# Reversing the order of the query blocks and starting the first group's first pass by chunks

## The chip, the core and the metric

The kernel runs on one core of a Trainium2 chip. The metric is the device time of one execution in microseconds (us), from the first to the last instruction and the little around them. A core has five engines that run side by side: TensorE (PE: matrix multiplies, with weight loads shown as PEld), VectorE (DVE), ScalarE (ACT), GpSimd (POOL) and SyncE (SP), which here only issues DMA transfers, in the order in which they are written. The profiler also records the clock that the chip grants to TensorE, as a share of full speed; in these traces it is either 1.0 or 0.5 at any moment, and means over a stretch lie between.

## The reference

Two layers over two sequences of 2048 tokens with 256 channels. What matters here is the first layer: a differential attention (16 heads, each a difference of two causal softmaxes with 8 channels) beside a mixture of experts (8 routed experts, two for each token, and one shared expert), both on the normalised input. The second layer (a state-space scan and a network with weights of plus and minus one) is not touched by the change.

```python
x = L0_attn_x                                   # (2, 2048, 256)
xn = _layernorm(x, axis=-1)
x = x + _L0_attn_ref(xn, ...) + _L0_ffn_ref(xn, ...)
xn = _layernorm(x, axis=-1)
x = x + _L1_attn_ref(xn, ...) + _L1_ffn_ref(xn, ...)
# in _L0_attn_ref
qkv = x @ w_attn
att = jnp.einsum('bhtd,bhsd->bhts', q, k) * (1.0 / math.sqrt(hd))
att = jnp.where(causal, att, -jnp.inf)
att = jax.nn.softmax(att, axis=-1)
att = att[:, :, 0] - lambda_full * att[:, :, 1]
out = jnp.einsum('bhts,bhsd->bhtd', att, v)
```

## The kernel before

Everything about the first layer is in `layer0`. A **block** is 512 tokens; a sequence `b` has four, T = 0 to 3, so there are eight, numbered 4b + T. A **group** is one block and one eighth of the heads (four score matrices, two heads). Causality makes a group of block T look at T + 1 blocks of keys ("chunks"): its keys are 4T + 4 tiles of 128. So there are 64 groups, and 2 x 8 x (4 + 8 + 12 + 16) = 640 steps of the second pass. One such step, a **unit**, is four score multiplies (L467), four exponentials on ACT (L474), and four multiplies with the values (L493, "av"). A unit is also the clock of the hand-written plan: `at` counts units.

Softmax needs the maximum of each row first. That is the **first pass** (`first_pass`): score multiplies with queries as weights (L395), the mask added by small bf16 multiplies on the diagonal (L409, "halves"), and a maximum on DVE over PSUM (L416). The negative maxima are turned (L432) and sent by a DMA into a row of the query tile, where the second pass adds them. The first pass of a group is spread over the units of the group before it.

`place(begin, end, steps)` spreads steps over a stretch of units; `until(time)` releases them between the scores. The order on PE and SP is exactly this order; the other engines are ordered by the tile framework. What is placed beside the attention:

- `prepare(blk)`: load a block of x, statistics, normalise, eight transposes, the router's logits (L271), and a store to `xnT`. Before: block 0 at the start, the others at units 4 blk - 7 to 4 blk - 3.
- `project_qk(b, T)` and `project_v(b, T)`: the projections of a block, just before its first group. Queries and keys are split into two float32r parts in a tile `parts` of one buffer (L318, L319), stored to a scratch (L325) and loaded again by groups (`load`, L367 and L372).
- `project_out`: the output projection of a block when its last group is done, added to x and stored in `x1`.
- `route()` and `scatter(n)`: the choice of experts at units 30 to 44, and the scatter of rows at units 46 to 108.
- `expert_steps()`: 55 jobs of 256 rows, 16 of the shared expert and 39 of routed ones, each five "visits" long (L809 up and gate, L831 down; together "MoE", all with the PSUM tile `moe`). Their visits are spread evenly from unit `BEGIN` = 48 to the end: 1320 multiplies, each two instructions in the trace. Four shared jobs (of the last two blocks) come after the routed ones.
- `gather(pair)`: near the end, for each of 16 pairs of tiles, an indirect DMA by POOL (L926) fetches the routed results and DVE adds them.

`NSH = NBLK - 2` marks the two blocks (6 and 7) whose shared jobs come last; block 7 (`NBLK - 1`) ends the layer, with its sum held in the tile `late`. After unit 640, `project_out` of the last block and the statistics end the layer; then the weights of layer 1 are loaded (`load_branch`, `load_signs`) and `layer1` runs.

Of the kernel before, what the change touches and what calls it, by code (L numbers as in the profile page):

```python
# [37 lines left out]
@with_exitstack  # L38
def block_kernel(ctx: ExitStack, tc: tile.TileContext, t: dict, out: bass.AP):
    nc = tc.nc  # L40

    x = t["L0_attn_x"]
    B, S, C = x.shape
    NT = B * S
    NTILE = NT // P
    out_t = out.flatten_outer_dims().rearrange("(n p) c -> p n c", p=P)


    const = ctx.enter_context(tc.tile_pool(name="const", bufs=1))
# [24 lines left out]

    def behind():
        normalisation(0, NTILE - 4)
        pool = w1p.enter_context(tc.tile_pool(name="w1", bufs=1, side="right"))
        load_branch(tc, t, pool, ident, w1)

    layer0(tc, t, x, x1, mv, rstd, ident, eps, behind)  # L80
    normalisation(NTILE - 4, NTILE)


    pool = w1p.enter_context(tc.tile_pool(name="w1f", bufs=1, side="right"))
    layer1(tc, t, B, S, x1, shift, rstd, ident, w1, out_t, lambda: load_signs(tc, t, pool, w1))
    w1p.close()


def layer0(tc, t, x, x1, mv, rstd, ident, eps, ended):
# [31 lines left out]
    with ExitStack() as ctx:  # L121
# [4 lines left out]
        def load_x(key, blk=None):  # L126
            blk = key if blk is None else blk
            xbs[key] = new(sp, [P, 4, C], "xb")
            nc.sync.dma_start(xbs[key], x_t[:, 4 * blk : 4 * blk + 4, :])

        load_x(0)
        load_x(1)
# [102 lines left out]
        def prepare(blk):  # L235
# [29 lines left out]
            def logits():  # L265
# [3 lines left out]
                for i in range(4):  # L269
                    for k in range(KC):  # L270
# [7 lines left out]
                if blk:  # L278
# [17 lines left out]
            for b in range(B)  # L296
        }

        def project_qk(b, T):

            blk = b * NTB + T
            heads = P // HD
# [21 lines left out]
                    d = dst[:, :, part] if n == "q" else dst[:, part]  # L324
                    nc.sync.dma_start(d, parts[:, part].bitcast(F32))  # L325

            return [lambda n=n, e=e: one(n, e) for e in range(KC) for n in "kq"]

        vas = {}

# [194 lines left out]
        def project_out(b, T, out):  # L525
# [3 lines left out]

            def scale():  # L530
                xbs[blk] = late
                if blk < NBLK - 1:
# [31 lines left out]
            def project(i):  # L564
                pt = new(ps1, [P, 2, 512], "s1")[:, 0]
                for k in range(KC):
                    nc.tensor.matmul(
                        pt[:, :C],
                        oTs[i][:, k * P : (k + 1) * P],
                        wo[:, k, :],  # L570
                        start=(k == 0),
                        stop=(k == KC - 1),
                    )
                acc = xbs[blk][:, i, :]
                nc.vector.tensor_tensor(acc, acc, pt[:, :C], ALU.add)
                if blk == NBLK - 1:
                    statistics(4 * blk + i, acc)

            def store():
                nc.sync.dma_start(x1[:, 4 * blk : 4 * blk + 4, :], xbs.pop(blk))  # L580
                projected.add(blk)

            steps = [scale]
            steps += [lambda: turn(0)]
# [2 lines left out]
            return steps + [store]  # L587


        stored, projected, begun = set(), set(), []  # L590
        NSH = NBLK - 2

        def statistics(n, acc):
            st = new(sp, [P, nc.vector.BN_STATS_DIM], "bnst", bufs=3)
# [161 lines left out]
        def expert_steps():  # L756
# [95 lines left out]
            def load_base(jb):  # L852
                n = GT * jb["j"]
                begun.append(n // 4)
                jb["c"] = new(mps[0], [P, GT, C], "c", bufs=2)
                src = x1 if n // 4 in projected else x_t
                nc.sync.dma_start(jb["c"], src[:, n : n + GT, :])
# [9 lines left out]

            def finish(jb):
                n = GT * jb["j"]
                if n // 4 < NBLK - 1:  # L870
                    for i in range(GT):
                        statistics(n + i, jb["c"][:, i, :])

            order = [dict(j=j, shared=True, last=False) for j in range(2 * NSH)]
            order += [dict(j=j, shared=False) for j in range(NJ)]
            order += [dict(j=j, shared=True, last=True) for j in range(2 * NSH, 2 * NBLK)]
            v = 0
            for i, jb in enumerate(order):
                names = ("gate", "up"), ("down",)
                begins = jb["j"] == (2 * NSH if jb.get("last") else 0)  # L880
                if not jb["shared"]:
                    if begins:
                        put(v, to_routed)
# [26 lines left out]
        def gather(pair):  # L910
# [1 line left out]
            n = GT * pair  # L912

            def load():
                if n // 4 < NBLK - 1:
# [19 lines left out]
            def add():  # L935
                for i in range(GT):
                    acc = pairs[pair][:, i, :]
                    for o in range(2):
# [4 lines left out]
                    if n // 4 < NSH:  # L943
                        statistics(n + i, acc)

            return load, add, (lambda: store_last(pair)) if n // 4 < NSH else None

        def store_last(pair):
            n = GT * pair
            acc = pairs.pop(pair)  # L950
            if n // 4 < NBLK - 1:
                nc.sync.dma_start(x1[:, n : n + GT, :], acc)

        pairs = {}
# [4 lines left out]
        LEAD, FETCH = 3, 2  # L959
        groups, at = [], 0  # L960
        for b in range(B):
            for T in range(NTB):
                for g in range(NG):
                    groups.append(dict(b=b, T=T, g=g, at=at, n=4 * T + 4))
                    at += 4 * T + 4
# [8 lines left out]
        for i, grp in enumerate(groups):  # L974
# [673 lines left out]
```

## Time and profile before

| | us |
|---|---|
| median of 9 runs | 4181.72 (4155.36 to 4214.71) |
| the profiled execution | 4169.49 |
| its span | 4167.8 |
| first second-pass score at | 77.5 |
| end of the attention, about | 2894.5 |
| first scan of layer 1, about | 2973 |

A "windows" view gives, for stretches of the span, how long each engine was busy (with the number of instructions), the mean granted clock and the DMA share; filtered by a line or a tile it counts those instructions alone. Counting L467 (four for each unit) tells which stretch of time holds which units: units 0 to 47 lie in 77.5 to 393.7 (193 of L467), the same 48 units of the second sequence (320 to 367) in 1527.4 to 1759.2 (192), units 528 to 591 in 2442.5 to 2673.9 (256), and the last 48 in 2673.9 to 2894.5 (192). A busy PE is not a fast PE: at half the clock the same multiply is busy about twice as long.

### The profile page before, as it was taken

The page shows a single profiled execution, that of the slowest core. Times are in us where ns is not written, and L with a number is a line of the kernel's source. Part 1 is how long each engine was busy: PE and PEld are TensorE (multiplying, and loading weights), DVE is VectorE, ACT ScalarE, POOL GpSimd, SP SyncE. Part 2 cuts the span into 40 slices and gives each one's busy share as a digit, 9 for nine tenths or more (in the row PEclk, how much of TensorE's full clock was granted, in tenths as well). Part 3 has the DMA queues.
Part 4 walks back from the last instruction along what each step waited for, and adds up shares of the span by engine and source line. Part 5 has one row for each costly group of instructions (what it writes and reads, how often), then busy time and mean ns, then how long its engine had stood idle before and what let it go on. Part 6 is the DMA issues. An engine that isn't in the chain of part 4 may idle for free. (4 is left out here: it accounts for less than half of the span.)

```text
span 4167.8 us, 58041 instructions
## 1 busy us (share of the span) xinstructions
PE 3726.0 (89%) x20976; PEld 1994.8 (48%) x20976; DVE 2771.0 (66%) x3758; ACT 2329.8 (56%) x4766; POOL 1488.7 (36%) x1859
## 2 busy tenths in 40 slices
PE   6789999999999999999999999987487887878888
PEld 3444444544444445554454454443254544545545
DVE  4355576756676535656666667673488888888888
ACT  2334444645665554555565556544575775776674
POOL 2112332101000022111110100142587887888887
PEclk7556997998999999999999999988698888889989
DMA  3322321112122322222222222332322322321331
GB/s 103 103 75 79 108 92 58 52 57 79 64 87 65 100 74 93 74 87 88 70 84 89 67 72 79 98 103 64 124 75 78 112 86 72 114 93 64 122 102 41
DMA packets 219022, 348.70 MB, mean 84 GB/s; under 512 B 31968, under 2 KB 118496, under 8 KB 218736
## 3 DMA queue, kind: packets, MB, share of 16 engines
q1 hardware_dynamic: 212048, 327.68, 23.8%
q0 software_dynamic: 6144, 16.79, 1.2%
q8 instruction: 167, 2.74, 0.3%
q14 instruction: 119, 0.97, 0.1%
q10 hardware_dynamic: 544, 0.52, 0.0%
HBM read 261.93 MB, written 82.31 MB: 83 GB/s over the span
## 5 line engine op out<-in xcount | busy, mean ns | idle before, releaser
L416 DVE TENSOR_REDUCE mpart<-s 128x2 f32<-128x1024 f32 (+3 forms) x1280 | 1353.0, 1064 | 667.8 <-PE s L467 335.0
L474 ACT ACTIVATE pr<-s 128x512 f32<-128x512 f32 (+3 forms) x2560 | 1248.8, 532 | 923.6 <-PE s L467 636.7
L467 PE MATMUL s<-qst,kc 34*128 34x512 f32 (+3 forms) x2560 | 1022.0, 466 | 42.9 <-ACT pr L474 28.3
L395 PE MATMUL s<-kc,qst 33*128 33x512 f32 (+3 forms) x2560 | 946.5, 449 | 50.0 <-DVE mpart L416 27.3
L478 POOL TENSOR_SCALAR_AFFINE_SELECT pr<-pr 128x128 f32<-128x128 f32 x1024 | 290.9, 293 | 1617.2 <-ACT pr L474 1604.4
L395 PEld LDWEIGHTS s<-kc,qst 33*128 33x128 f32 x2560 | 432.1, 203 | 744.1 <-issue 319.9
L493 PE MATMUL av<-pr,va 128*17 128x512 f32 (+3 forms) x5120 | 653.8, 582 | 4.6 <-POOL pr L478 4.6
L1519 POOL TENSOR_TENSOR u<-dxr,bc 128x1024 f32<-128x1024 f32 x256 | 601.6, 2371 | 12.5 <-DMA bc<-bcd 12.5
L467 PEld LDWEIGHTS s<-qst,kc 34*128 34x128 f32 x2560 | 448.2, 200 | 171.5 <-ACT pr L474 98.8
L1532 ACT ACTIVATE a<-dtr,w_A 128x512 f32<-128x512 f32 x512 | 350.7, 691 | 169.0 <-DVE u L1579 150.2
L1418 PEld LDWEIGHTS f<-h,w_f 128*128 128x128 f32 x2048 | 262.1, 196 | 102.3 <-issue 35.0
L1579 DVE TENSOR_TENSOR_SCAN a<-a,state,u 128x512 f32<-128x512 f32 x240 | 307.0, 1279 | 3.6 <-ACT a L1532 2.7
L1418 PE MATMUL f<-h,w_f 128*128 128x256 f32 x2048 | 288.6, 297 | 16.2 <-ACT h L1425 9.3
L409 PE MATMUL s<-halves 64*128 64x128 bf16 x2048 | 288.7, 242 | 0.0
L809 PE MATMUL moe<-xT,w_up 128*128 128x256 f32 x880 | 266.6, 428 | 0.0
L809 PE MATMUL moe<-xT,w_gate 128*128 128x256 f32 x880 | 265.7, 427 | 0.0
L1418 PE MATMUL f<-xhl,w_f 128*128 128x256 f32 x512 | 121.6, 368 | 133.8 <-DVE h L1429 99.4
L1585 DVE TENSOR_TENSOR u<-a,bc 128x512 f32<-128x512 f32 x320 | 221.4, 692 | 14.4 <-DVE a L1579 0.5
L1593 POOL TENSOR_TENSOR u<-u,bc 128x1024 f32<-128x1024 f32 x96 | 227.1, 2366 | 7.7
L831 PE MATMUL moe<-w_down,hT 128*128 128x256 f32 x880 | 224.2, 399 | 0.0
L1544 PE MATMUL y<-u,w_sel 128*32 128x512 f32 x1024 | 190.1, 655 | 33.4 <-POOL u L1593 27.7
L519 POOL TENSOR_TENSOR ao<-n 128x128 f32<-128x128 f32 x64 | 29.4, 459 | 526.8 <-DVE n L516 526.0
(196 smaller groups left out, 4196.9 us busy)
## 6 DMA issues: line engine op xcount, KB each, us to landing
kc<-kd SPq DMA_DIRECT2D x640, 64.0 KB
dxr<-dtd SPq DMA_DIRECT2D x64, 512.0 KB
dtr<-dtd SPq DMA_DIRECT2D x64, 512.0 KB
w_gate<-in_L_ffn_gate_proj_w SPq DMA_DIRECT2D x39, 512.0 KB
w_up<-in_L_ffn_up_proj_w SPq DMA_DIRECT2D x39, 512.0 KB
w_down<-in_L_ffn_down_proj_w SPq DMA_DIRECT2D x39, 512.0 KB
qst<-qd SPq DMA_DIRECT2D x256, 64.0 KB
bc<-bcd SPq DMA_DIRECT2D x32, 512.0 KB
```

The costliest lines, as they stand in the source:

```text
L395: nc.tensor.matmul(pt[:, i, :width], grp["q"][r : r + R + 1, pair, tt * P : (tt + 1) * P], grp["k"][ch][r : r + R + 1, pair, :width], star ...
L409: nc.tensor.matmul(pt[:, head, tt * P : width], halves[h, 0, half, :], halves[h, 1, half, :], start=False, stop=half == 1,)
L416: nc.vector.tensor_reduce(grp["mpart"][:, tt, 2 * pair : 2 * pair + 2, ch : ch + 1], pt[:, :, :width], AX.X, ALU.max,)
L467: nc.tensor.matmul(pt[:, lo:], grp["k"][st // 4][r : r + R + 2, pair, (st % 4) * P : (st % 4 + 1) * P], grp["q"][r : r + R + 2, pair, lo:] ...
L474: nc.scalar.activation(pr[:, j, lo:], pt[:, lo:], AF.Exp)
L478: nc.gpsimd.affine_select(out=block, in_=block, compare_op=ALU.is_ge, fill=0.0, base=0, pattern=[[1, P]], channel_multiplier=-1,)
L493: nc.tensor.matmul(av[32 * j : 32 * j + DV + 1, lo:], vas[b, st // 4][:, st % 4, 2 * g + j // 2, :], pr[:, j, lo:], start=(st == 0), stop= ...
L809: nc.tensor.matmul(moe[:, half, :], w[:, k, m * P : (m + 1) * P], jb["xT"][:, k, :], start=(k == 0), stop=(k == KC - 1),)
L1418: nc.tensor.matmul(pt, w[wname][:, k, m * P : (m + 1) * P], h[src][:, k, part, :], start=(k + part == 0), stop=(k + 1 + part == nk + 1),)
L1519: nc.gpsimd.tensor_tensor(u, sg["dxr", c, half], sg["bc", g][:, 0:1, :].to_broadcast([P, 2, L]), ALU.mult)
L1532: nc.scalar.activation(a, sg["dtr", c, half][:, i, :], AF.Exp, scale=w["A"][:, k : k + 1])
L1579: nc.vector.tensor_tensor_scan(h, a, u[:, i, :], sg["before"]["state"][:, k[i] : k[i] + 1] if sg["before"] else 0.0, ALU.mult, ALU.add,)
```

## The change

The plan is rearranged; the multiplies, exponentials and maxima are the same in number and shape.

- The blocks of each sequence run T = 3, 2, 1, 0. So the first group of a sequence needs the keys of all four blocks.
- For sequence 0 the beginning is new: block 3 is prepared and its q and k projected, then for T = 0, 1, 2 the block is prepared and its k projected, and the first group's first pass runs by chunks in between. v of all four blocks and q of blocks 0 to 2 are placed beside that first pass (which reads the blocks again from `xnT` with `load_xT`).
- The four blocks of sequence 1 are prepared at units 2 to 21 and projected at units 190, 212, 236 and 293, over 16 units each.
- The expert visits begin at unit -10 in place of 48.
- The blocks whose shared jobs come last are now 4 and 5 (T = 0 and 1 of sequence 1): `LAST` and `NEXT`. The order of the gathers follows.
- The second layer's normalisation is made in three pieces in place of two.

```diff
     def behind():
-        normalisation(0, NTILE - 4)
+        normalisation(0, 16)
+        normalisation(20, NTILE)
...
-        def project_qk(b, T):
+        def project_qk(b, T, names="kq"):
...
-            return [lambda n=n, e=e: one(n, e) for e in range(KC) for n in "kq"]
+            return [lambda n=n, e=e: one(n, e) for e in range(KC) for n in names]
...
-        NSH = NBLK - 2
+        LAST, NEXT = NBLK - NTB, NBLK - NTB + 1
+        ended_by = [LAST, NEXT]
...
-            order = [dict(j=j, shared=True, last=False) for j in range(2 * NSH)]
+            ends = [GT * blk + i for blk in ended_by for i in range(2)]
+            order = [dict(j=j, shared=True, last=False) for j in range(2 * NBLK) if j not in ends]
             order += [dict(j=j, shared=False) for j in range(NJ)]
-            order += [dict(j=j, shared=True, last=True) for j in range(2 * NSH, 2 * NBLK)]
+            order += [dict(j=j, shared=True, last=True) for j in ends]
...
         for b in range(B):
-            for T in range(NTB):
+            for T in reversed(range(NTB)):
...
-                b, T = grp["b"], grp["T"]
                 grp["out"] = {}
-                before = project_qk(b, T) + project_v(b, T)
-                start = begin - FETCH - 2 - 2 * len(before)
-                place(start, begin - FETCH - 2, before)
-                if i:
-                    place(start - 3, start - 3, [lambda blk=b * NTB + T: load_xT(blk)])
...
-                place(end + 5, end + 14, project_out(grp["b"], grp["T"], grp["out"]))
-
-        place(-60, -59, prepare(0))
-        for blk in range(1, NBLK):
-            place(4 * blk - 7, 4 * blk - 3, prepare(blk))
+                soon = (grp["b"], grp["T"]) == (B - 1, 1)
+                place(end + 5, end + (10 if soon else 14), project_out(grp["b"], grp["T"], grp["out"]))
+
+        last = NTB - 1
+        for i, T in enumerate([last] + list(range(last))):
+            start = 4 * max(i - 2, 0) + (-22 if i > 1 else 2 * i - 40)
+            place(start, start + 0.5, prepare(T))
+            place(start + 0.5, start + 1, project_qk(0, T, "kq" if T == last else "k"))
+            start = 4 * T - 15
+            place(start, start, [lambda T=T: load_xT(T)])
+            place(start + 0.5, start + 3.5, project_v(0, T) + (project_qk(0, T, "q") if T < last else []))
+            place(5 * i + 2, 5 * i + 6, prepare(NTB + last - i))
+        for T, start in enumerate((190, 212, 236, 293)):
+            place(start - 3, start - 3, [lambda blk=NTB + T: load_xT(blk)])
+            place(start, start + 16, project_qk(1, T) + project_v(1, T))
...
-        BEGIN = 48
+        BEGIN = -10
...
-        pairs_order = [12, 0, 1, 2, 13, 3, 4, 14, 5, 6, 15, 7, 8, 9, 10, 11]
+        pairs_order = [8, 0, 1, 2, 3, 9, 4, 5, 6, 7, 12, 13, 14, 15, 10, 11]
...
+            if pair // 2 == NEXT:
+                time = at - 20.5 + pair % 2
```

More of the change, by code (lines that the diff above doesn't have):

```diff
@@ L80, in block_kernel @@
     layer0(tc, t, x, x1, mv, rstd, ident, eps, behind)
-    normalisation(NTILE - 4, NTILE)
+    normalisation(16, 20)
     pool = w1p.enter_context(tc.tile_pool(name="w1f", bufs=1, side="right"))
@@ L129, in load_x @@
             nc.sync.dma_start(xbs[key], x_t[:, 4 * blk : 4 * blk + 4, :])
+        load_x(NTB - 1)
         load_x(0)
-        load_x(1)
         wqk = new(wp, [P, KC, 2 * C], "wqk")
@@ L277, in logits @@
                         )
-                if blk:
+                if blk >= NTB:
                     xTs.pop(blk)
@@ L531, in scale @@
                 xbs[blk] = late
-                if blk < NBLK - 1:
+                projecting.add(blk)
+                if blk != LAST:
                     assert begun.count(blk) == 2 * (blk in stored)
@@ L575, in project @@
                 nc.vector.tensor_tensor(acc, acc, pt[:, :C], ALU.add)
-                if blk == NBLK - 1:
+                if blk == LAST:
                     statistics(4 * blk + i, acc)
@@ L581, in store @@
                 projected.add(blk)
+                projecting.remove(blk)
             steps = [scale]
@@ L587, in project_out @@
             return steps + [store]
-        stored, projected, begun = set(), set(), []
-        NSH = NBLK - 2
+        stored, projected, projecting, begun = set(), set(), set(), []
+        LAST, NEXT = NBLK - NTB, NBLK - NTB + 1
+        ended_by = [LAST, NEXT]
         def statistics(n, acc):
@@ L854, in load_base @@
                 begun.append(n // 4)
+                assert n // 4 not in projecting
                 jb["c"] = new(mps[0], [P, GT, C], "c", bufs=2)
@@ L869, in finish @@
                 n = GT * jb["j"]
-                if n // 4 < NBLK - 1:
+                if n // 4 != LAST:
                     for i in range(GT):
                         statistics(n + i, jb["c"][:, i, :])
-            order = [dict(j=j, shared=True, last=False) for j in range(2 * NSH)]
+            ends = [GT * blk + i for blk in ended_by for i in range(2)]
+            order = [dict(j=j, shared=True, last=False) for j in range(2 * NBLK) if j not in ends]
             order += [dict(j=j, shared=False) for j in range(NJ)]
-            order += [dict(j=j, shared=True, last=True) for j in range(2 * NSH, 2 * NBLK)]
+            order += [dict(j=j, shared=True, last=True) for j in ends]
             v = 0
@@ L879, in expert_steps @@
                 names = ("gate", "up"), ("down",)
-                begins = jb["j"] == (2 * NSH if jb.get("last") else 0)
+                begins = jb["j"] == (ends[0] if jb.get("last") else 0)
                 if not jb["shared"]:
@@ L914, in load @@
             def load():
-                if n // 4 < NBLK - 1:
+                if n // 4 != LAST:
                     assert n // 4 in projected
@@ L942, in add @@
                         )
-                    if n // 4 < NSH:
+                    if n // 4 not in ended_by:
                         statistics(n + i, acc)
-            return load, add, (lambda: store_last(pair)) if n // 4 < NSH else None
+            return load, add, (lambda: store_last(pair)) if n // 4 not in ended_by else None
         def store_last(pair):
@@ L950, in store_last @@
             acc = pairs.pop(pair)
-            if n // 4 < NBLK - 1:
+            if n // 4 != LAST:
                 nc.sync.dma_start(x1[:, n : n + GT, :], acc)
```

## The prediction, made before the changed kernel was run

> **What bounds the kernel now.** I read the page's slices first, then the windows by stage, then the start's timeline. Of the 40 slices (104 us each), this is PE, its granted clock, and DVE:
>
> ```profile
> PE   6789999999999999999999999987487887878888
> ...
> DVE  4355576756676535656666667673488888888888
> ...
> PEclk7556997998999999999999999988698888889989
> ```
>
> PE is the full engine from slice 4 to slice 26, the first layer. But in slices 1 to 3 it is 70 to 90% busy at about half the clock. The windows give that by stage (columns: stretch, its length, busy us and instructions of PE, PEld, DVE, ACT and POOL, granted clock, DMA share, GB/s):
>
> ```profile
> 0.00:77.50 77.50, 41.59 (x167) 25.07 (x167) 34.45 (x67) 9.94 (x18) 18.01 (x35) 0.79 0.29 93
> 77.50:393.70 316.20, 271.06 (x1326) 142.33 (x1325) 150.28 (x299) 121.24 (x257) 54.50 (x173) 0.54 0.26 86
> ...
> 1527.40:1759.20 231.80, 218.41 (x1449) 122.79 (x1448) 130.04 (x203) 113.24 (x265) 58.76 (x180) 0.91 0.30 92
> ...
> 2442.50:2673.90 231.40, 229.68 (x1489) 114.14 (x1488) 164.28 (x193) 147.79 (x306) 19.86 (x68) 1.00 0.24 78
> 2673.90:2894.50 220.60, 194.63 (x989) 89.08 (x992) 119.25 (x236) 109.50 (x218) 76.44 (x113) 0.84 0.33 96
> ```
>
> Rows two and three hold the same 48 units of the two sequences: 316.2 us against 231.8, although the later ones carry MoE too. Row four is the dense stretch: 64 units, PE busy throughout, full clock. Two more windows, of all instructions:
>
> ```profile
> 393.70:2894.50 2500.80, 2402.57 (x14582) 1208.77 (x14586) 1552.19 (x2084) 1377.28 (x2905) 419.56 (x1079) 0.93 0.25 80
> 626.00:671.00 45.00, 39.72 (x158) 18.62 (x158) 19.50 (x29) 17.09 (x30) 15.57 (x20) 0.51 0.20 68
> 172.00:380.00 208.00, 187.62 (x894) 98.91 (x891) 104.42 (x208) 79.53 (x168) 36.22 (x111) 0.50 0.23 79
> ```
>
> From 172 to 380 PE was busy 187.62 of 208 us, at half clock all the while, and rose when MoE began. So PE's being busy is not what raises the clock here; multiplies that fill the array are (MoE 128x128; the scores have 33 or 34 rows, the values 17 columns). MoE alone, by the same windows:
>
> ```profile
> 77.50:393.70 316.20, 0.00 (x0) 0.00 (x0) 0.00 (x0) 0.00 (x0) 0.54 0.26 86
> 1527.40:1759.20 231.80, 62.60 (x213) 39.68 (x212) 15.51 (x37) 10.26 (x27) 0.91 0.30 92
> ```
>
> **The sum.** The built orders hold the same PE work, so I ask what it costs where it now stands. Unit prices at full clock, from starts to next starts in the timeline (instructions of the trace): MoE .24 us (four from 2600.46 to 2601.43), q or k projection .48 (four from 2210.30 to 2212.21), v projection .27 (four from 2249.78 to 2250.85), transpose .13 (four from 2601.43 to 2601.96), score .14 and mask .07 (four each from 2601.96 to 2602.79). A logit instruction took .22 at half clock (14 in 3.15 us), so .11.
>
> *1. MoE from unit -10: the clock of the first units.* 231.8 less 213 MoE at .24 (51) is 181 without MoE. The first 48 units of before also held six preparations (48 transposes, 96 logits: 17 us) and lacked seven sets of four routed turns (4 us): 194. They took 316: **-122** for running this work at the later clock. MoE itself is moved, not added. Bounds: -142 (also the rest of the clock, 0.91 to 1.00) and -60 (half of the early units still slow).
>
> *2. The longer start.* The timeline of before:
>
> ```profile
> 32.10 0.60 ACT L318 ACTIVATE parts<-s 128x512 fp32r<-128x512 f32 x1 [3.19 <-PE s L310]
> 36.36 0.60 ACT L318 ACTIVATE parts<-s 128x512 fp32r<-128x512 f32 x1 [3.66 <-DMA kd<-parts]
> 39.86 0.60 ACT L318 ACTIVATE parts<-s 128x512 fp32r<-128x512 f32 x1 [2.90 <-DMA qd<-parts]
> ...
> 48.71 0.60 SPq L372 DMA_DIRECT2D kc<-kd  x1
> ...
> 53.87 0.57 PE L395 MATMUL s<-kc,qst 33*128 33x128 f32 x2 [5.26 <-DMA kc<-kd]
> ```
>
> A projection waits for the store of the one before, as `parts` has one buffer: 4 us each. A first score waits 5.2 us for its chunk. In the changed order, before the first chunk's loads SP stands behind eight projections: four of block 3 (32 to 48), two of block 0 (to 58), then block 1's x is loaded only behind those stores (3), gets its statistics and is normalised (4.6, as from 17.4 to 22.0 before), is turned, copied and given its logits (6.3, as from 22.0 to 28.3), and two projections and their stores follow (10): 82. The loads take 8 x .65 = 5 us of SP's issue, first scores at 88. Block 2's x stands behind them (88), and chunk 1 behind block 2's k stores: another 3 + 5 + 6 + 10 + 5 = 29 us, 117. From there PE is dense: 48 scores, 64 v, 24 q instructions, 32 masks, 40 MoE: 7 + 17 + 12 + 2 + 10 = 48 us at full clock, 96 at half. v, q and MoE fill the array, so nearer the first: 53, and first second-pass score at **170** (150 to 215), +92. In exchange this left the later units: 48 q and k (23), 48 v (13), 48 scores (7), 16 transposes and 32 logits (5), 40 MoE (10), less 24 masks (2): -56. Net **+36** (+16 to +81). Queued behind these waits on SP are the first MoE weights, and MoE is only due in the third chunk.
>
> *3. Thinner MoE.* The 1320 MoE multiplies now go over 650 units, not 592. In the built orders, units without any MoE are 42 from unit 48 on before, 99 in all after: 57 more. What does an empty unit cost? From 393.7 to 2894.5 the mean clock is .93, so 14% of 2501 us at half clock, 175 us lost. If all of it came from the 42 empty units: 4.2 us each. The stretch at 626 began in one (unit 100) and ran 45 us at half clock. The low end is 0: the dense stretch has four empty units and clock 1.00. Two thirds of the units are T = 3 and 2 groups like it, a third has the projections, steps between blocks, or T = 1 and 0; nearer the low end, **1.1 us, +63** (0 to +239).
>
> *4. Steps between blocks.* The first pass of a longer block runs in fewer units. Of the second sequence, the last two groups before T = 3 took 108.4 us for 24 units where two plain ones took 87.0; four us of it is extra scores and v, 17 are waits. Before T = 2 about 4, before T = 1 some 15 (1640.7 to 1669.9: 7.3 us a unit). The old order has these upward steps in both sequences; beyond the 48 units of point 1 they come to 17 + 4 + 36 = 57. The new order has one, T = 0 to 3, with 32 DVE maxima of 1.06 us in four units: 34 us where some 16 were, and DVE's other work: 33 or so. **-20** (-40 to +10).
>
> *5. The end.* The last 48 units took 220.6 us against 174 at the dense rate: 47 lost beside the gathers. The new last units (T = 1, 0) have POOL's masks (L478) in every unit, in POOL's order behind gathers that wait for DVE; a late mask holds the values on PE. Where a step is slower another was removed (no projections, few first passes): **0** (-20 to +47). The transition to layer 1, 78.5 us, and layer 1, 1194.8 us, are the same instructions: 0.
>
> -122 + 36 + 63 - 20 = **-43 us** on 4167.8. The profiled run (4169.5) lies 12 below the median, so 4181.7 - 43 = **4139**.
>
> [...]
>
> **Rivals.** *A, slower: empty units cost most of the lost clock.* 3.2 us each gives +182 in place of +63: +76, **4258**. For it: 626 to 671, and that they are now every seventh unit, often beside narrow diagonal units; against it: the dense stretch. It decides from 1.85 us each on. *B, empty units harmless*, .2 us each: +11, -95, **4087**. For it: the dense stretch, and that the projections' v and q also fill the array. *C, the start eats it*: each chunk exposed and at half clock, first score at 215: +45 on the forecast, **4184**. For it: one `parts` buffer, SP's order; against: v and q stand between the scores.
>
> **Numbers.** Forecast .45, A .27, B .2, C .08. The likeliest one's own range is 4105 to 4170. The range over all: **4060 to 4225**, which leaves out the far half of A and little of B. A measurement of this kernel tells .5% (21 us) from no change: faster .55 (most of the forecast, all of B), same .16 (the forecast's end, C), slower .29 (A and the end of C).
>
> **What would show it.** Clock near 1 from the first units on; first second-pass score near 170; projections 4 us apart at the start; low clock beside no more than a quarter of the empty units; units 312 to 315 taking some 30 us. Wrong if the mean clock of the attention falls below .93, if the first score comes after 215, or if the last T = 0 groups take over 25 us each.

## The result, and the profile after

The changed kernel is slower: 4280.53 us (median of 20 runs, 4228.2 to 4316.41) against 4175.08 for the kernel before, run beside it. The ratio is 1.0226, with a 95% interval of 1.0198 to 1.0253. The profiled execution took 4260.44 us and has a span of 4258.7, against 4167.8. The forecast was 4139, with a range up to 4225.

The median of the kernel before lay between 4131 and 4173 in the four sets of runs below. So kernels are compared by their ratio to runs of before made beside them, and the single profiles are used to find where time went. A profile can lie some tens of us from the median of its kernel's runs (31 below and 38 above at most in the runs below).

The slices of the page after (106 us each; PE, granted clock):

```profile
PE 3780.3 (89%) x20976; PEld 2010.8 (47%) x20976; DVE 2773.4 (65%) x3760; ACT 2328.8 (55%) x4769; POOL 1489.6 (35%) x1859
PE   4799999999999998999999999988388787888888
...
PEclk7566898997899896999999889979689898899989
```

The clock still starts low (the second to fourth slice), and the tenth and sixteenth slice now have .7 and .6, where the page before had .8 and .9. The windows of after by the same stages as before (up to the first second-pass score, units 0 to 47, units 48 to 639, units 312 to 315; the columns are those of the prediction's windows):

```profile
0.00:242.90 242.90, 155.35 (x376) 81.33 (x376) 86.33 (x142) 30.69 (x57) 18.01 (x35) 0.65 0.27 88
242.90:498.00 255.10, 246.10 (x1163) 121.55 (x1162) 154.17 (x260) 119.10 (x233) 14.56 (x50) 0.72 0.25 82
498.00:2987.60 2489.60, 2370.11 (x14535) 1196.50 (x14535) 1500.58 (x2049) 1357.40 (x2891) 460.42 (x1201) 0.91 0.24 78
1624.30:1670.00 45.70, 34.09 (x129) 15.41 (x128) 32.83 (x33) 8.38 (x20) 5.13 (x17) 0.59 0.24 78
```

and of the MoE's instructions alone:

```profile
0.00:242.90 242.90, 18.25 (x40) 11.08 (x40) 3.36 (x8) 1.53 (x4) 0.65 0.27 88
242.90:498.00 255.10, 70.84 (x201) 43.71 (x200) 17.11 (x41) 6.13 (x16) 0.72 0.25 82
498.00:2987.60 2489.60, 700.35 (x2401) 443.88 (x2400) 176.83 (x423) 105.72 (x278) 0.91 0.24 78
```

Against before: the start is 165.4 us longer (242.9 for 77.5), units 0 to 47 are 61.1 shorter (255.1 for 316.2), units 48 to 639 are 11 shorter (2489.6 for 2500.7), and what follows the attention is 2 shorter: +91 in all. Two things stand out. The start is far longer than the 170 foreseen. And units 48 to 639 lost 241 MoE instructions to earlier places (58 us at the prediction's .24 each) and are only 11 us shorter.

Where the start goes shows in its timeline. Each line is: start, us, engine, line, instruction, [idle before and what ended it]:

```profile
86.33 0.89 PE L396 MATMUL s<-kc,qst 33*128 33x512 f32 x2 [9.56 <-DMA kc<-kd]
...
120.61 1.64 PE L396 MATMUL s<-kc,qst 33*128 33x512 f32 x3 [2.42 <-DMA kc<-kd]
```

The chain of prepare, project, store and load behaved as foreseen: first scores at 86.3 (foreseen 88), chunk 1 at 120.6 (foreseen 117). The rest of the first pass, priced at 53 us, took 122. A piece of it:

```profile
157.56 2.05 PE L342 MATMUL s<-wv,xTb 128*128 128x256 f32 x4 [3.91 <-DMA xTb<-xnT]
159.54 1.32 PE L396 MATMUL s<-kc,qst 33*128 33x512 f32 x2
161.65 2.07 PE L342 MATMUL s<-wv,xTb 128*128 128x256 f32 x4 [0.79 <-DVE mpart L417]
```

Four instructions of v take 2.05 us (half clock), and the next ones wait for a maximum on DVE. v, q and the score pairs all take their PSUM tiles from the pool of two named `s1`, so each must wait until the reader of that tile's last use is done, and for a score pair that is the maximum on DVE.

### The profile page after: what moved, and what is told of

Read it like the earlier page. It is cut to its first block, busy times and chain, and to the rows that moved or that the text cites. A ratio compares the mean times of both kernels' runs of the same rounds, so it can differ in the third digit from the quotient of the medians.

```text
span 4258.7 us, 58031 instructions
## 1 busy us (share of the span) xinstructions
PE 3780.3 (89%) x20976; PEld 2010.8 (47%) x20976; DVE 2773.4 (65%) x3760; ACT 2328.8 (55%) x4769; POOL 1489.6 (35%) x1859
## 5 line engine op out<-in xcount | busy, mean ns | idle before, releaser
L468 PE MATMUL s<-qst,kc 34*128 34x512 f32 (+3 forms) x2560 | 1029.5, 466 | 31.9 <-ACT pr L475 24.2
L396 PE MATMUL s<-kc,qst 33*128 33x512 f32 (+3 forms) x2560 | 966.6, 455 | 90.6 <-DVE mpart L417 46.2
L1434 PE MATMUL f<-h,w_f 128*128 128x256 f32 x2048 | 283.0, 293 | 18.1 <-ACT h L1441 11.1
L410 PE MATMUL s<-halves 64*128 64x128 bf16 x2048 | 278.7, 233 | 0.0
L814 PE MATMUL moe<-xT,w_up 128*128 128x256 f32 x880 | 278.4, 443 | 0.0
L814 PE MATMUL moe<-xT,w_gate 128*128 128x256 f32 x880 | 278.3, 443 | 0.0
L836 PE MATMUL moe<-w_down,hT 128*128 128x256 f32 x880 | 232.8, 411 | 0.0
```

Source lines behind the costliest of these rows:

```text
L396: nc.tensor.matmul(pt[:, i, :width], grp["q"][r : r + R + 1, pair, tt * P : (tt + 1) * P], grp["k"][ch][r : r + R + 1, pair, :width], star ...
L410: nc.tensor.matmul(pt[:, head, tt * P : width], halves[h, 0, half, :], halves[h, 1, half, :], start=False, stop=half == 1,)
L468: nc.tensor.matmul(pt[:, lo:], grp["k"][st // 4][r : r + R + 2, pair, (st % 4) * P : (st % 4 + 1) * P], grp["q"][r : r + R + 2, pair, lo:] ...
L814: nc.tensor.matmul(moe[:, half, :], w[:, k, m * P : (m + 1) * P], jb["xT"][:, k, :], start=(k == 0), stop=(k == KC - 1),)
L1434: nc.tensor.matmul(pt, w[wname][:, k, m * P : (m + 1) * P], h[src][:, k, part, :], start=(k + part == 0), stop=(k + 1 + part == nk + 1),)
```

## The experiments

The names are plain: *new order* is the changed kernel's order of blocks with its start; *late MoE* is `BEGIN` = 48, *early MoE* is -10.

**Early MoE in the old order.** One number of the kernel before:

```diff
-        BEGIN = 48
+        BEGIN = -10
```

> The old order of blocks with the expert visits from unit -10, nothing else. Theory S (a clock that is at half needs far more array-filling work to rise than one that is full needs to stay; the changed kernel lost its time between 117 and 434 us because it was at half clock there): the first units of the old order have PE waits and short groups, so the clock rises late here too, but before 380; the first 48 units take 300 to 340 us with MoE in them (316 before without), and the total is 40 to 80 us below the kernel before, as MoE has left the later units. Rival V (empty units between MoE visits lose the clock all over): 99 empty units as in the changed kernel, so the mean clock of the attention after unit 48 falls below .91 and the total is no better than before, 4170 or more.

Ratio 1.0172 (1.0100 to 1.0245). The windows of units 0 to 47 and 48 to 639:

```profile
91.50:422.40 330.90, 296.87 (x1524) 165.93 (x1524) 167.82 (x339) 125.64 (x273) 54.76 (x174) 0.70 0.27 87
422.40:2958.10 2535.70, 2418.10 (x14343) 1198.31 (x14346) 1532.88 (x2034) 1370.25 (x2883) 419.45 (x1077) 0.90 0.24 77
```

The first units ran at clock .70 (.54 before) and are 15 us longer (316.2 before): what the clock gave, the added MoE work used up. The later ones are 35 us longer (2500.7 before), although MoE work had left them. The start is longer too, by 14 us (91.5 for 77.5), as the first visits now stand in it. Of the two theories V holds: the clock after unit 48 is .90 and the total is no better than before. S had the length of the first units right, and the total wrong; what it supposes of the work that a clock needs to rise and to stay is shown by no run.

**Late MoE in the new order.** `BEGIN` = 48 in the changed kernel, with the shared jobs starting from block 3, whose x is ready:

> The changed kernel with the expert visits from unit 48 as before (the shared jobs of block 3 are put first, as its projection comes early now). Theory S: without MoE the whole stretch from the start to unit 48 stays at half clock: first second-pass score near 225 (20 MoE instructions fewer at half clock, 243 in the changed kernel), units 0 to 47 at about 5.5 us, 265 us; later units as dense as before with 42 empty ones. Total 4270 to 4330. Rival V: the later units gain more than the first ones lose, total below 4230.

Ratio 1.0124 (1.0045 to 1.0203), against after's 1.0226. The same two windows:

```profile
231.80:487.20 255.40, 235.15 (x965) 104.77 (x964) 139.06 (x219) 115.29 (x218) 14.21 (x48) 0.51 0.23 76
487.20:2973.90 2486.70, 2402.43 (x14776) 1231.12 (x14779) 1521.46 (x2099) 1365.60 (x2912) 462.26 (x1203) 0.92 0.25 79
```

Units 0 to 47 took 255.4 us at clock .51; in after they took 255.1 at .72, with 201 MoE instructions that were busy 70.8 us. PE's other work fell from 235.2 to 175.3 us (246.1 - 70.8), by about as much. So MoE runs there free of charge, and shortens nothing. Units 48 to 639 took 2486.7 with nearly all of the MoE in them; in after, with 241 instructions of 2640 gone, 2489.6. The total is V's (4217 is below 4230). One caution for what follows: this profile (4244.79) is the longest of the four runs of this kernel, 28 us above their median, and after's is 20 us below its own.

**Dummy multiplies in the new start.** 46 multiplies of 128 x 128 by 256, never read, before unit -10:

```diff
+        for time, n in ((-25, 14), (-20.5, 14), (-17.99, 8), (-15.01, 4), (-13, 2), (-12, 2), (-11, 2)):
+            place(time, time, [lambda n=n: warm(n)])
```

> The changed kernel with 46 added multiplies of 128x128 by 256 columns (float32, two instructions each) into the still unused MoE tile, placed in the waits of the start, before unit -10; their results are used by nothing. Theory S: they lift the clock before the chunks; from 120 us on the clock is near 1, the first second-pass score comes at 180 to 195 in place of 243, groups 0 and 1 take 70 and 60 us in place of 112 and 79; total 4140 to 4180, 80 to 120 us below the changed kernel, although work was added. Rival P (the start is long because score pairs and projections take turns with DVE's maxima through two PSUM tiles, and because of the parts buffer and SP's order): the clock may rise, but the first score stays after 230 and the total within 20 us of the changed kernel or above it.

First second-pass score at 237.2, 6 earlier; ratio 1.0242 (1.0186 to 1.0298). The clock rose only in places (.61, .56 and .75 in the three stretches of 30 us from 120 on; .56, .50 and .52 in after), so these dummies hardly shorten this start, as rival P had it.

**Dummy multiplies in the old first units.** Two in each of the units -4 to 47 of before:

> The kernel before with two added multiplies of 128x128 by 256 columns (float32, two instructions each, 0.96 us at full clock) at the end of each unit from -4 to 47, into the still unused MoE tile; nothing uses them. Theory S: the clock rises within the first 60 us after the first score; the first 48 units take 240 to 270 us in place of 316, total 4105 to 4135: faster by adding 50 us of work. Rival P: the first groups are bound by waits among the engines, the added 50 us come on top, total 4200 or more.

Ratio 1.0063 (1.0006 to 1.0120). Units 0 to 47 took 325.6 us at .68 (316.2 at .54 before); over the whole profiled execution the clock was .893 (.883 before). As with the MoE, the clock rises, the added work uses it up, and the time doesn't fall. S wanted 240 to 270 us; P was nearer, though the total, 4189, is under its 4200.

**Own PSUM tiles for v and q in the start.** The changed kernel with

```diff
+                if b == 0:
+                    pt = new(ps2, [P, 512], "s2")
+                else:
                     pt = new(ps1, [P, 2, 512], "s1")[:, 0]
```

in `project_v`, and the same in `project_qk` for q alone.

> The kernel after, with one edit: the values of the first sequence and the q of its blocks 0 to 2 are multiplied into the two one-bank tiles that the second pass's scores use (idle before the first of them) and not into the two tiles that the first pass's score pairs, whose maxima VectorE takes, turn through. Between 120 and 243 us of the kernel after, TensorE waited 8.9 + 5.2 + 2.2 = some 16 us before the score pairs, the values and q, of which 13 for the maxima, and was at half clock. Theory R (the turn of two tiles makes the start long): the waits for maxima in this stretch fall from 13 us to under 4, TensorE is busy without gaps, its clock rises before 210 us, first second-pass score at 180 to 215 us (243 in after), time 4215 to 4250. Theory C (TensorE's own work at half clock makes it long: 32.7 + 32.6 + 17.9 + 18.1 + 4.7 = 106 of 122 us are its busy time): the waits go but the clock stays near .55, first score at 225 to 240, time 4262 to 4281.

Ratio 1.0180 (1.0128 to 1.0232), first score at 217.0. Windows of the stretch from 120 us to the first second-pass score, of after and then of this kernel:

```profile
120.00:242.90 122.90, 99.36 (x224) 49.90 (x224) 40.19 (x45) 11.32 (x27) 0.00 (x0) 0.57 0.21 72
```

```profile
120.00:217.00 97.00, 74.02 (x224) 39.79 (x224) 39.87 (x46) 11.23 (x27) 0.00 (x0) 0.73 0.27 91
```

The same 224 instructions are busy 74 us and not 99, at clock .73 and not .57. What PE waited for in these stretches (us in total, times, the longest), again of after and then of this kernel:

```profile
PE s L342 <- DMA xTb<-xnT: 8.8, 4, 3.9
PE s L396 <- DVE mpart L417: 6.0, 5, 1.3
PE s L342 <- DVE mpart L417: 5.2, 7, 0.8
...
PE s L311 <- DVE mpart L417: 2.2, 3, 0.8
```

```profile
PE s L348 <- DMA xTb<-xnT: 18.7, 4, 7.5
PE s L402 <- DVE mpart L423: 2.9, 4, 1.1
```

The waits for maxima fall from 13.4 to 2.9 us. In the timeline the pieces now follow each other, and v takes 1.13 us:

```profile
154.72 0.50 PE L402 MATMUL s<-kc,qst 33*128 33x512 f32 x1
155.15 1.13 PE L348 MATMUL s<-wv,xTb 128*128 128x256 f32 x4
156.21 0.49 PE L402 MATMUL s<-kc,qst 33*128 33x512 f32 x2
```

Theory R holds in its waits and its clock, but the first score is just outside its range (217 against 180 to 215) and PE still has gaps: the loads of `xTb` come first now. PE's idle time is the same in both stretches (122.9 - 99.4 = 23.5 us and 97.0 - 74.0 = 23.0), so nearly all of the 26 us gained is busy time of the same instructions, which goes with the clock. Why the clock rose with the other tiles is not shown.

**A lean start.** The new order with late MoE, v in the tiles `s2`, and q of blocks 0 to 2 out of the start:

```diff
-            place(start + 0.5, start + 3.5, project_v(0, T) + (project_qk(0, T, "q") if T < last else []))
+            place(start + 0.5, start + 3.5, project_v(0, T))
+            if T < last:
+                start = 40 * (last - T) + 20
+                place(start - 3, start - 3, [lambda T=T: load_xT(T)])
+                place(start, start + 8, project_qk(0, T, "q"))
```

> The new order with the MoE from unit 48 (measured 4217 as it stood), with less in the start: the values of the first sequence go into the tiles of the second pass's scores, and q of blocks 0 to 2 (24 multiplies, 17.9 us in after's stretch of 120 to 243) is computed at units 60, 100 and 140 from columns loaded again. Its first second-pass score stood at 231.8 us. Theory C (the start is TensorE's work at half clock, so work taken out of it comes back at the full clock and is worth half of its time): first score at 205 to 215, units 48 to 639 longer by some 9, time 4195 to 4208. Theory R (without waits for the two tiles the clock rises as well): first score at 170 to 195, time 4160 to 4185. If what is taken out of the start comes back in the same length later: 4212 to 4220.

Ratio 1.0001 (0.9961 to 1.0042): 0.0123 below the new order with late MoE, as fast as before. First score at 181.0, 51 us earlier. But theory R is only half right, as the window shows:

```profile
120.00:181.00 61.00, 55.76 (x158) 30.11 (x157) 31.76 (x31) 5.84 (x16) 0.00 (x0) 0.50 0.20 64
```

PE is busy nine tenths of the time (55.8 of 61 us) and the clock stays at half. Nor does it do what the prediction expected of v beside the scores: the 64 instructions of v, 128 x 128, are some 33 us of the 55.8 busy (an estimate from the 2.07 us that four take at half clock in after), and the clock stayed at .50. With q and MoE between the scores (the experiment above) it was .73, without them .50. The edit changes the tiles and takes q out at once, so the 51 us aren't divided between the two.

**MoE steps not rounded to ends of units.** In the changed kernel `time = when(visit)` without the rounding.

> The kernel after, with one edit: the MoE's steps keep their own times and are not moved to the end of the unit they fall in, so that they spread over the quarters of all units and the empty units (99 of 640 by the rounding) take part of their neighbours' work; the amount of MoE work is the same. Theory V (units without MoE lose the clock, and with it time: thin MoE from unit -10 costs some 60 us): mean clock of units 48 to 639 rises from .91 to over .93, these units 2430 to 2465 us (2490 in after), time 4225 to 4260. Theory M (the mean share of MoE over a stretch sets the clock, not the holes): units 48 to 639 within 10 us of 2490, time 4270 to 4290. If steps in mid-unit hold the scores up (TensorE waits for the MoE's tiles there): slower than 4300.

Ratio 1.0866 (1.0786 to 1.0945): the third case, and more so. Second-pass scores waited 72.9 us for exponentials, in 215 places (24.2 us in 50 before the edit). The edit changes two things at once, the spread and the waits, so it says nothing on empty units.

**Filled holes.** The changed kernel with two multiplies, never read, at the end of each of the 98 units that have no MoE work:

```diff
+        filled = {math.floor(when(visit)) for visit in full}
+        for u in range(BEGIN, at - 2):
+            if u not in filled:
+                place(u + 0.995, u + 0.995, [lambda: warm(2)])
```

> The kernel after, with two added multiplies (128 x 128 by 256, their result is never read) at the end of each of the 98 units from -10 on that have no MoE work: 196 multiplies. From the old order, where 104 such multiplies in units -4 to 47 cost 10 to 20 us, and the MoE's own 1320 multiplies at 1142 us of records (.87 us each, partly overlapped), this is 50 to 100 us of TensorE work added to a stream that has it busy nine tenths of the time. Theory V (an empty unit loses the clock; filled, it does not): clock from unit 48 on rises from .91 to .95 or more, which gives back what the multiplies take: 4240 to 4290. Theory M (holes do not matter): clock as before, time 4330 to 4380.

Ratio 1.0279 (1.0215 to 1.0343), so the 196 multiplies cost some 20 us by the ratio (1.0279 less 1.0226), where 50 to 100 us of work had been added; the interval holds after's ratio too. The window of units 48 to 639, all instructions:

```profile
489.00:2928.20 2439.20, 2347.36 (x14897) 1213.65 (x14900) 1501.72 (x2049) 1354.18 (x2891) 461.25 (x1201) 0.95 0.25 79
```

With 362 instructions more than after, PE is busy 23 us less, the clock is .95 and not .91, and in this profile the units are 50 us shorter. But this profile (4203.81) is the shortest of its kernel's four runs, 31 us below their median, so it overstates that. By the ratio nothing is gained, but most of the multiplies' price is paid back. That speaks for theory V: 1.0279 of 4175 is 4291, at the end of its range, while M's 4330 to 4380 lies above the whole interval.

The trace of after says the same, counted from the starts of the scores and the granted clock, from unit 48 on. Where the unit ahead ran at over .95, the clock fell in the unit or in the one after it 18 times of 81 where the unit had no MoE, and 23 times of 356 where it and the unit ahead had MoE.

**Denser MoE in the old order.** `BEGIN` = 96 in the kernel before, which leaves 5 units without MoE from there on.

> The kernel before with one number changed: the MoE begins at unit 96 and not at 48. The same multiplies then stand in 544 units instead of 592 and, by the rounding, 5 units from there on have none (40 in before, 98 in after, where it begins at -10); the old order with -10 measured 1.0172 of before. Theory V (units without MoE work lose the clock, and the time with it; MoE in the first units gains nothing): the trend goes on, with 35 units without MoE fewer at the .6 us that the step from 48 to -10 gives for each of 58 (some 34 us against the 48 units that now stand empty in a row at half clock, before unit 96): 4130 to 4160, clock from unit 96 on .95 or more. Theory W (what costs in the early start is only that MoE work stands in the start and the first units, where it slows the chain): from 48 on there is nothing to gain, and units 48 to 95 empty while the rest is denser: 4170 to 4190.

Ratio 1.0065 (1.0033 to 1.0097): a miss for both. The windows of units 48 to 95 and 96 to 639, of before and then of this kernel:

```profile
393.70:606.80 213.10, 204.35 (x1260) 103.90 (x1260) 139.40 (x202) 104.78 (x232) 75.55 (x152) 0.94 0.30 103
606.80:2894.40 2287.60, 2198.12 (x13323) 1104.79 (x13326) 1412.79 (x1883) 1272.45 (x2672) 344.01 (x927) 0.93 0.24 78
```

```profile
395.20:629.10 233.90, 219.13 (x1045) 94.81 (x1045) 123.69 (x157) 100.64 (x214) 76.83 (x150) 0.56 0.24 83
629.10:2873.70 2244.60, 2175.81 (x13534) 1112.88 (x13533) 1429.89 (x1928) 1277.19 (x2692) 345.50 (x929) 0.97 0.25 81
```

V's clock came (.97), its time didn't. By the profiles the denser units gained 43 us and the emptied ones lost 21; but the two profiles can't be set against each other so closely. This one (4136.42) is 17 us below the median of its runs, in a set in which before's median was 4136, and before's profile (4169.49) is from a set in which it was 4182. By the ratio the loss is 27 us of 4175. So of -10, 48 and 96, the 48 of before is the best, and thinning is not the only thing that counts.

**The old start with the second sequence reversed.** The first sequence as before, the second with T = 3, 2, 1, 0, projected at units 190 to 320. Of the edit, made in the changed kernel, this is the line of the order; the others put back the start and the preparations of the kernel before:

```diff
-            for T in reversed(range(NTB)):
+            for T in range(NTB) if b == 0 else reversed(range(NTB)):
```

It was run with late MoE, with early MoE, and with late MoE and its 40 empty units filled, and was expected, in this order:

> First sequence with blocks first to last and the start of the kernel before, second sequence last to first, MoE from unit 48 as before: the step from block 3 of the first sequence to block 0 of the second (units 312 to 321) is gone, the start is the old one, and q, k and values of the second sequence are projected in units 190 to 320. From the new order with late MoE, the second sequence measured 1281 us (483.9 + 368.1 + 286.9 + 141.8) against 1367 in before (160.0 + 283.3 + 401.1 + 522.7), of which the projections of its blocks 1 to 3, some 3 times 20 us, are moved into the first sequence. Theory S (the start alone makes the new order slower, the rest of the new order gains): 4130 to 4160. Theory O (the order of blocks changes nothing but where work stands): 4165 to 4185, with the second sequence shorter by what the first gets longer.

> The kernel with the old first sequence and the second one from last to first (0.9843 of before, with the MoE from unit 48), its MoE from unit -10 as in after. Theory V (early, thin MoE costs by itself, whatever the order: 0.010 between after and the new order with late MoE, 0.017 in the old order): ratio to before 0.994 to 1.004, clock from unit 48 on .01 to .03 lower. Theory O (it costs only where it stands beside a crowded start): the new order's start is gone here, ratio 0.980 to 0.990.

> The same kernel with the MoE from unit 48 and two multiplies, never read, in each of the 40 units from 48 on that have no MoE work (80 multiplies, 40 us of TensorE at half a microsecond each). Theory V (the holes cost the clock): clock of units 48 to 639 rises by .01 to .02 and gives back what the multiplies take or more, ratio 0.975 to 0.986. Theory M (holes do not matter): ratio 0.990 to 0.995.

| | ratio to before | 95% interval |
|---|---|---|
| late MoE | 0.9843 | 0.9790 to 0.9896 |
| early MoE | 1.0089 | 1.0046 to 1.0132 |
| late MoE, holes filled | 0.9907 | 0.9876 to 0.9938 |

The first, 4113.68 us where before took 4172.70, beats both kernels, and by more than theory S had foreseen (4130 to 4160). Early MoE costs 0.025 in this order too, so theory V holds of its two, though 1.0089 is above its range. Its profile shows what the old order did: first score at 91.4, units 0 to 47 in 330.8 us at .70 (.879 over the whole execution, .877 in the old order). Filling the holes gained nothing over the first: the intervals meet, V's range ended at .986, and .9907 lies in that of theory M, for which holes do not matter. The windows of units 48 to 639, of the first and then of the filled one:

```profile
391.90:2877.50 2485.60, 2402.92 (x14582) 1210.68 (x14585) 1557.28 (x2086) 1380.90 (x2908) 421.77 (x1079) 0.93 0.25 81
```

```profile
396.90:2821.70 2424.80, 2356.55 (x14742) 1202.11 (x14746) 1555.71 (x2086) 1377.67 (x2907) 419.76 (x1079) 0.96 0.26 84
```

Again 160 instructions more, a higher clock and less busy time; but the profile of the first was the longest of its five runs (4151.89), so the 61 us between the two overstate it. Over all runs the mean clock of the execution was .891 without and .900 with filled holes, while that of before, in the same two sets, was .881 and .887: more than half of the difference is that of the sets. So in this order the runs don't show that holes cost anything.

## Why the prediction was wrong

The span grew by 91 us where -43 was foreseen. The steps that failed are point 1's -122, the gain from running the first units at the later clock, which the visits did not bring, and point 2's 53 us for the rest of the first pass, which took 122. Term by term, by the profiles:

| term of the sum | foreseen | measured | from |
|---|---|---|---|
| early MoE in the units (points 1 and 3) | -122 + 63 = -59 | +3 | units 0 to 639 of after less those with late MoE: 2744.7 - 2742.1 |
| longer start (point 2) | +92 | +165 | 242.9 - 77.5 |
| work that left the later units, and the steps (2, 4, 5) | -56 - 20 + 0 = -76 | -75 | units 0 to 639 with late MoE less before: 2742.1 - 2816.9 |
| after the attention | 0 | -2 | 1271.1 - 1273.4 |

The first and the third row use the profile of late MoE, which was long for its kernel. By the ratios early MoE costs 43 us in this order, where the two profiles lie only 16 apart (4258.7 - 4243.1). An estimate that puts the missing 27 us into the units makes the first row +30 and the third -102; the sum stays.

**Point 1 failed.** The step was "-122 for running this work at the later clock", with MoE counted as moved. MoE raised the clock of the first units to .72, not to the .91 of the row it was compared with, and the work that raised it used up what it gave: 255.1 us with and 255.4 without in the new order, 330.9 and 316.2 in the old one, 325.6 with dummies. What early MoE did gain there is its own 201 instructions, 48 us at .24 each. The 61 us by which these units are shorter than before came with the order alone (255.4 with late MoE): the projections of blocks 1 to 3 and the steps between blocks are no longer there, and that was booked in point 2. The reading under the step was not exact either. In before the half clock of the row from 172 us on gave way to the full one at 380.1, after four multiplies of an output projection at 377.6, for 13.7 us; MoE's first multiply came at 396.9, and the next rise at 400.6. With 128 x 128 multiplies added the mean clock of the first units was .72 and .70 (MoE) and .68 (dummies); in the lean start, with those of v, it was .50. So it isn't shown that the form of a multiply is what raises the clock.

**Point 3 was right in sign and, as far as the runs tell, too small.** In the old order early MoE made units 48 to 639 35 us longer while 58 us of MoE left them: 93 us over 50 more units without MoE, 1.9 each (the prediction's 57 count seven of units 0 to 47 too). In the new order it is (3 + 58) / 50 = 1.2 by the profiles, and 1.8 with the 27 us above. The term was 1.1. That it is the empty units that cost this is supported by the filled holes in the new order, and not by those in the kernel with the old start, so it isn't shown. With point 1 gone, early MoE costs by the ratios 0.017, 0.010 and 0.025 in the three orders (72, 43 and 103 us of 4175), each uncertain by 0.007 to 0.008. Some of it stands in the start, which the early visits make longer by 14 us in the old order (91.5 for 77.5) and by 11 in the new one (242.9 for 231.8).

**Point 2 was mis-sized.** The chain up to chunk 1 was right to 4 us. The term "PE is dense: ... 53" was wrong: PE had the work, but v and q went through the same two PSUM tiles as the score pairs, whose release comes from DVE, and the clock was .57. The price was put nearer to full clock because of the 128 x 128 multiplies of v, q and MoE; of 122.9 us PE was busy 99.4, for 48 at full clock in the sum, and idle 23.5, so the low clock is the larger part of the miss. Own tiles gave 26 us of the 70 missed, nearly all of it in busy time; own tiles with q out of the start gave 51 where the MoE was late. In that lean start v is by the estimate above more than half of the busy time and the clock stayed at .50, so the reason given for the price doesn't hold there. What keeps the clock at half stays open.

**Points 4 and 5, with the work that left the later units, came out as a sum** by the profiles, -75 for -76. With the 27 us above it would be -102, so the close agreement is luck. The one step from T = 0 to T = 3 was dearer than foreseen (units 312 to 315 took 45.7 us at clock .59, DVE busy 32.8 of it, foreseen some 30). Which other terms were cheaper is not shown. The last eight groups took 18.1 us each, well under the 25 that were named as a sign of trouble.

By ratios the loss can be taken back in two steps: late MoE takes 0.0102 off the 1.0226, and the lean start on top of it another 0.0123, which leaves 1.0001. What is left, the reversal with a first score at 181.0 against 77.5, is then neither gain nor loss.

**The rivals.** A's 4258 is 22 us below the measured median, and it comes so near by luck: it wanted 3.2 us for each empty unit, where the runs give 1.2 to 1.9, and kept point 1's gain. C, the start as what eats the gain, had the right place with the smallest chance; it named late chunks, and it was the rest of the first pass, with its two tiles and a low clock. B, empty units harmless, would need early MoE to gain, and it lost in all three orders; the filled holes speak against it in the new order and leave it open with the old start. Of the signs that were named, the mean clock of the attention (.72 and .91 in its two stretches) and the first score after 215 both spoke against the forecast.

## What to carry to other kernels

Here work that was moved to raise the clock used up what the clock gave (255.1 us with it, 255.4 without), and the clock came to .72, not to the .91 counted on: count such work, look up the clock that it really brings, and price the units that it leaves. Before work is put between the steps of a chain, look at the buffers that it turns through: here v and q in the tiles of the score pairs meant 13.4 us of waits for their maxima, and 2.9 in tiles of their own. A reordering is best tried by halves: here the second sequence's half alone gained 0.016 (ratio 0.9843), and the first one's start gave that away.

## What was not expected of the hardware

- With the v multiplies and the scores alone (the lean start, 120 to 181 us), PE 91% busy, the clock stayed at .50 for 61 us; with q and MoE among them (own tiles, 120 to 217 us), PE 76% busy, its mean was .73. Of these two stretches, both with 128 x 128 multiplies, the busier one had the lower clock.
- With 196 more multiplies PE's busy time was less, 2347.4 us for 2370.1 in units 48 to 639, at a clock of .95 for .91. These are two single profiles, the first of them from the shortest of four runs; over whole executions the clock was .884 to .901 in those four, and .861 to .882 in the runs of after.
- The mean clock of a run differs between runs of one kernel, and the time with it: of ten runs of the lean start, eight took 4162.8 to 4174.0 us at .876 to .881, and two took 4206.9 and 4208.1 at .867 and .868. The longest and the shortest are 1.1% apart, so a difference under 1% can't be read from two profiles of it.
